# A GRU on one core: filler matmuls ahead of z's product in step 0, and smaller loads at the start

## The chip, the cores and the metric

One core of a Trainium2 chip runs the program. The metric is device time in microseconds (us), the median of several executions. The engines are named as in the profile: PE is TensorE (matmuls; PEld its weight loads), DVE is VectorE, ACT is ScalarE, POOL is GpSimd, SP is SyncE, which issues nearly all DMAs. A "q" behind an engine's name means its instruction queue.

## The reference

A gated recurrent unit runs over 128 time steps of `x` with 64 batch rows and 512 features, and its states are added to `x`:

```python
def step(h, inp):
    x_t, prop = inp
    comb = jnp.concatenate([x_t, h], axis=-1)
    z = jax.nn.sigmoid(comb @ Wz + bz)
    r = jax.nn.sigmoid(comb @ Wr + br)
    comb2 = jnp.concatenate([x_t, r * h], axis=-1)
    h_cand = jnp.tanh(comb2 @ Wh + bh)
    h_new = (1.0 - z) * h + z * h_cand
    h_next = jnp.where(prop, jnp.tanh(h_new @ Wp + bp), h_new)
    return (h_next, h_new)
# result: x + the sequence of h_new
```

`prop` holds at every fourth step but the last. Each of Wr, Wz, Wh is 1024 x 512 float32: the upper 512 rows meet x (input weights), the lower 512 meet h or r*h (state weights).

## The kernel before

A 64 x 512 state is kept as a tile of 128 partitions and 256 columns: the two halves of the features lie one below the other (`S = 2`, `B = 64`, `N = 256`). Before it can be multiplied, a tile is turned: `turn` makes eight small transposes on PE for both of its column blocks (`C = 2`) and another engine copies the result out of PSUM. `turn_x(t)` does that for step t's x, with ACT as the copying engine unless another is given.

`product(ps, lT, w, k)` is the unit of matrix work: one 128-row block k of a weight against one turned block, as two matmuls for the two halves, which the profile shows as four matmul records. A product over a whole weight takes four units in the order `ORDER = [0, 2, 1, 3]`.

What depends on x alone does not depend on the recurrence. It is cut into units that stand in `queue`, and `fill(n)` runs the next n of them, so that PE has work while the other engines bring r, z and h along. A list's last unit leaves a closure in `pending`; `read_out()` runs it, which adds the biases on DVE and writes the sums to `cp` (L435 and L440). For steps 0 to 3 the units are `plain(t)`: four of r, four of z, four of the candidate (gate order R, Z, H_). From step 4 on a scheme with fewer multiplications (Strassen-like, over several steps) is used. It needs sums of weight blocks, which DVE and POOL make during steps 0 to 2: `sum_outer` (L319 to L321, six DVE operations), `sum_outer_1` (L325), `sum_inner` (L328 to L330, on POOL) and `sum_inner_1` (L333).

One step issues, in program order on each engine: r's product (`rc`), r's sigmoid on ACT (L751) and `rh = r * h` on DVE (L752); z's product (`zp`) with the turn of rh before its last unit; z's sigmoids on ACT (L775, L776) and `keep = (1 - z) * h` on DVE (L777); `fill(places[0])`; the candidate's product into `rc`; `read_out`; tanh on ACT (L808), `h = z * tanh + keep` on DVE (L809, L814); five units of filler; the turn of h's two halves, with one unit between them; the other units. `seed` (L410) copies the x part of a sum into PSUM before a product is added to it. In step 0 `sum_outer` stands in DVE's order right after `keep`, before `read_out` and h.

The order on each engine is the program's order (`manual_schedule`), and an engine waits in order. At the start SP issues the loads in the order in which they are written:

```python
    for i in (Z, H_):
        for k in (0, 2):
            load_w(wx[:, :, i, :], gates_in[i], k, k + 2, nc.sync)
    ...
    for i in range(3):
        for k in (0, 2):
            load_w(wh[i], gates_in[i][D:, :], k, k + 2, nc.sync)
        if i == 0:
            load_x(xr[0], 2, 2, 2)
```

Here `wx` holds the input weights, `wh[i]` the state weights of gate i, and `xr[0]` the first four steps of x. `load_x` (L95) makes two DMAs, one for each half of the features; `load_w` (L100) makes one. Ahead of these lines come steps 0 and 1 of x (L115) and r's input weights in four loads of 256 KB. Behind them come `load_xs` (L157, sixteen loads of another layout of x for steps 4 to 11), Wp, bp and the next x. SP's loads share eight semaphores in turn: a load is issued when the load eight places ahead of it has landed.

Of the kernel before, what the change touches and what calls it, by code (L numbers as in the profile page):

```python
# [17 lines left out]
def kernel(  # L18
# [29 lines left out]
    nc = tc.nc  # L48
    B, T, D = x.shape
# [10 lines left out]
    R, Z, H_ = range(3)  # L60
# [21 lines left out]
    wx = const.tile([P, K, 3, H], F32, name="wx")  # L82
    wh = [const.tile([P, K, H], F32, name=f"wh_{i}") for i in range(3)]
# [4 lines left out]
    gates_in = (Wr, Wz, Wh)  # L88
# [4 lines left out]
    def load_x(tile_, t0, n, j=0):  # L93
        for s in range(S):
            nc.sync.dma_start(  # L95
                out=tile_[s * B : (s + 1) * B, j : j + n, :], in_=x[:, t0 : t0 + n, ts(s, N)]
            )

    def load_w(wt, w, k0, k1, eng):
        eng.dma_start(  # L100
            out=wt[:, k0:k1, :],
            in_=w[k0 * P : k1 * P, :].rearrange("(k p) n -> p k n", p=P),
        )

    ORDER = [s * C + c for c in range(C) for s in range(S)]
    xr = {}
# [10 lines left out]
        )  # L117
    for k in ORDER:
        load_w(wx[:, :, R, :], Wr, k, k + 1, nc.sync)
    for i in (Z, H_):  # L120
        for k in (0, 2):
            load_w(wx[:, :, i, :], gates_in[i], k, k + 2, nc.sync)

    def load_bias(i, eng):
        for s in range(S):
# [12 lines left out]
    for s in range(S):  # L138
        nc.gpsimd.dma_start(out=h_init[s * B : (s + 1) * B, :], in_=h0[:, ts(s, N)])
    for i in range(3):  # L140
        for k in (0, 2):
            load_w(wh[i], gates_in[i][D:, :], k, k + 2, nc.sync)
        if i == 0:
            load_x(xr[0], 2, 2, 2)

    dummy = const.tile([1, 1], F32, name="dummy")
    nc.scalar.activation(dummy, ones[:, 0:1], AF.Sigmoid)
# [74 lines left out]
    def products(ps, lhs, rhs, start=False):  # L222

        for s in range(S):
            nc.tensor.matmul(  # L225
                ps[s * B : (s + 1) * B],
                lhsT=lhs,
                rhs=rhs(s),
                start=start,
                stop=True,  # L230
                skip_group_check=True,
            )

    def product(ps, lT, w, k, start=False):
        s0, c0 = divmod(k, C)
        products(ps, lT[:, c0, ts(s0, B)], lambda s: w[:, k, ts(s, N)], start)
# [4 lines left out]
    def turn(src, dst, c, name, eng):  # L241


        pt = turn_ps[c][:, :P].bitcast(BF16).rearrange("p (w n) -> p w n", w=2)
        for s in range(S):
            words = src[:, c * P + s * B : c * P + (s + 1) * B].bitcast(BF16)
            for w in range(2):
                nc.tensor.transpose(  # L248
                    pt[s * B : (s + 1) * B, w, :],
                    words.rearrange("p (n w) -> p w n", w=2)[:, w, :],  # L250
                    ident16,
                )
        copy(
            eng,
            dst[:, c, :].bitcast(U16).rearrange("p (n w) -> p n w", w=2),
            pt.bitcast(U16).rearrange("p w n -> p n w"),
        )
# [7 lines left out]
    def new_xT(g):  # L265
        if g not in xT:
            xT[g] = xtp.tile([P, Q4, C, P], F32, tag="xT", name=f"xT_{g}")

    def turn_x(t, eng=nc.scalar):
        g, i = divmod(t, Q4)  # L270
        new_xT(g)
        src = xr[g]
        for c in range(C):
            turn(src[:, i, :], xT[g][:, i], c, f"xT_{t}", eng)
# [141 lines left out]
    def fill(n):  # L416
        for _ in range(min(n, len(queue))):
            unit, end = queue.pop(0)
            unit()
            if end is not None:  # L420
                pending.append(end)
# [5 lines left out]
    def plain(t):  # L427

        first, second = scratch[:2] if t % 2 == 0 else scratch[2:]
        regions = (first[:, :N], first[:, N:], second[:, :N])  # L430
        g, i = divmod(t, Q4)

        def end():
            new_cp(t // 2)
            nc.vector.tensor_add(  # L435
                G[t][:, :, 0:2, :],
                first.rearrange("p (g c n) -> p c g n", g=2, c=C),
                bias[:, :, 0:2, :],
            )
            nc.vector.tensor_add(G[t][:, :, 2, :], cut(second[:, :N]), bias[:, :, 2, :])  # L440


        order = [(e, k) for e in range(3) for k in ORDER]
        if t == Q4 - 1:
            order = [(e, k) for k in ORDER for e in range(3)]
        units = [
            lambda e=e, k=k: product(
                regions[e], xT[g][:, i], wx[:, :, e, :], k, k == ORDER[0] and e != Z
            )
            for e, k in order  # L450
        ]
        return [(u, None) for u in units[:-1]] + [(units[-1], end)]
# [113 lines left out]
    def batches(g):  # L566

        if g * Q4 >= T:
            return []
        ms = [(g, i) for i in (1, 2, 6, 5, 7, 3, 4)]  # L570
        if g + 1 < LAST:
            ms += [(g + 1, i) for i in (1, 6, 2, 5, 3, 7, 4)]
        return sum((batch((g, n), ms[2 * n : 2 * n + 2]) for n in range(7) if 2 * n < len(ms)), [])
# [103 lines left out]
    for t in range(T):  # L677
# [6 lines left out]
        places = PLACES[u]  # L684
        if t == 0:
            queue.extend(plain(2) + plain(3))
            places = (12, 12)
        elif t == 1:
            queue.extend(batch((1, 0), [(1, 1), (1, 2)]))
            places = (8, 6)  # L690
        elif t == 2:
            queue.extend(batch((1, 1), [(1, 10), (1, 11)]) + batch((1, 2), [(1, 8), (1, 9)]))
            places = (12, 8)
        elif t == 3:
            queue.extend(batches(FIRST))
            places = (8, 8, 6)
        elif u == 7:

            queue.extend(batches(even + 2))
        thin = t >= T - 9  # L700
        if thin:

            places, behind = TAIL[t - (T - 9)]
        if t == T - 10:
# [7 lines left out]
            places = (4, 5)  # L712
# [13 lines left out]


        for k in ORDER:
            product(slots[R], hT, wh[R], k)
        if t < 2:  # L730
            if t == 0:
                turn_x(2)
        if t == 1:
            for i in (5, 7):
                sum_inner(i, nc.gpsimd)
# [19 lines left out]
            seed(H_, t)  # L755
        join(0)

        if t in (2, 3):
            fill((16, 6)[t - 2])


        for k in ORDER[: 2 if thin else 3]:
# [133 lines left out]
        n = 0  # L896
        if t >= T - CHUNK:
            n = {T - 2: 3, T - 1: 1}.get(t, 0)
        elif j == Q4 - 1:
            n = 4  # L900
# [56 lines left out]
```

## Time and profile before

| | |
|---|---|
| median of 3 runs | 1329.04 us (1328.59 to 1329.49) |
| the profiled execution | 1330.24 us, its span 1328.5 us |
| granted clock of TensorE, mean | 0.999 |
| busy: PE, DVE, ACT, POOL | 1319.2, 750.8, 554.4, 881.5 us |
| HBM read, written | 43.00 MB, 16.78 MB |

The span runs from the first to the last instruction; the execution's own time also holds what lies around it. A busy PE is not a PE at its peak, since matmuls are pipelined and their ends are modelled: one shown with 379 ns is followed by the next after about 108 ns. The timeline gives the start, the length, then engine, line, operation and tiles, and in brackets the idle time before it with what ended it.

### The profile page before, as it was taken

How to read it: one execution, taken by the hardware profiler on the slowest of the kernel's cores; microseconds unless marked ns; L12 is line 12 of the kernel's file. 1: busy time of each engine (PE TensorE's matmuls, PEld its weight loads, DVE VectorE, ACT ScalarE, POOL GpSimd, SP SyncE). 2: the span in 40 equal slices, each digit the busy share in tenths (PEclk: the TensorE clock that was granted, in tenths of full speed). 3: DMA queues.
4: the chain of work that ended last, by engine and by line, in shares of the span. 5: the costliest groups of instructions: out<-in, count | busy, mean ns of one | idle time of the engine just before them, and what ended most of it. 6: DMA issues, size and time to landing. Idle time of an engine off the chain costs nothing.

```text
span 1328.5 us, 37727 instructions
## 1 busy us (share of the span) xinstructions
PE 1319.2 (99%) x15312; PEld 1117.0 (84%) x15312; DVE 750.8 (57%) x2000; ACT 554.4 (42%) x1733; POOL 881.5 (66%) x1032
## 2 busy tenths in 40 slices
PE   9999999999999999999999999999999999999998
PEld 5888888888888888888888888888888888888865
DVE  3655555555555555555555555555555555555544
ACT  1344444444444444444444444444444444444433
POOL 4876766766767577675777757676676676757530
PEclk9999999999999999999999999999999999999999
DMA  8421122121121221222111221212212112121030
GB/s 236 90 50 30 21 49 49 33 49 34 33 49 33 54 45 18 49 43 56 33 33 34 50 49 34 47 20 49 49 34 49 34 33 49 33 49 33 18 104 17
DMA packets 171438, 62.22 MB, mean 47 GB/s; under 512 B 133600, under 2 KB 166496, under 8 KB 171264
## 3 DMA queue, kind: packets, MB, share of 16 engines
q1 hardware_dynamic: 170880, 59.47, 20.8%
q8 instruction: 121, 1.98, 0.6%
q14 instruction: 53, 0.43, 0.1%
q10 hardware_dynamic: 224, 0.20, 0.1%
q0 software_dynamic: 160, 0.14, 0.0%
HBM read 43.00 MB, written 16.78 MB: 45 GB/s over the span
## 4 chain that ended last, share of the span: by engine, by line
PE 96%; SPq 1%; DMA 1%; DVE 0%; issue 0%; ACT 0%; DVEq 0%; ACTq 0%
PE rc L225 33%; PE zp L225 20%; PE scratch_q L225 11%; PE scratch_r L225 11%; PE scratch_x L225 11%; PE scratch_a L225 5%; PE turn L248 5%; DMA xr<-in_x_dram 1%; SPq L157 1%; SPq L100 0%; DMA bias<-in_L_cond_bp_dram 0%; DVE wx L333 0%; DVE turn L809 0%; SPq L115 0%; DVE xT L281 0%
## 5 line engine op out<-in xcount | busy, mean ns | idle before, releaser
L225 PE MATMUL rc<-wh,rhT 128*64 128x256 f32 x2048 | 246.0, 379 | 0.0
L580 POOL TENSOR_TENSOR cp<-mb,mb 128x768 f32<-128x768 f32 x75 | 136.3, 1818 | 107.4 <-ACT rc L410 47.5
L225 PE MATMUL zp<-wh,hT 128*64 128x256 f32 x1536 | 204.6, 379 | 0.0
L225 PEld LDWEIGHTS rc<-wh,rhT 128*64 128x64 f32 x2048 | 168.6, 137 | 40.1
L225 PE MATMUL rc<-wh,hT 128*64 128x256 f32 x1536 | 186.5, 383 | 0.4
L891 POOL TENSOR_TENSOR xr<-xr,h 128x256 f32<-128x256 f32 x127 | 92.7, 730 | 126.3 <-DVE h L814 126.3
L225 PEld LDWEIGHTS rc<-wh,hT 128*64 128x64 f32 x1536 | 122.3, 137 | 36.1 <-issue 10.1
L580 POOL TENSOR_TENSOR cp<-mb 128x768 f32<-128x768 f32 x47 | 85.3, 1815 | 94.7 <-DVE h L814 89.8
L225 PEld LDWEIGHTS zp<-wh,hT 128*64 128x64 f32 x1536 | 119.7, 137 | 24.7
L809 DVE TENSOR_TENSOR turn<-turn,z 128x128 f32<-128x128 f32 x256 | 75.4, 295 | 102.2 <-ACT turn L808 100.7
L239 DVE COPY rhT<-turn 128x256 uint16<-128x256 uint16 x256 | 97.6, 420 | 56.0 <-PE turn L248 51.6
L751 ACT ACTIVATE turn<-rc 128x128 f32<-128x128 f32 x256 | 55.3, 260 | 171.4 <-issue 113.8
L239 ACT COPY hT<-turn 128x256 uint16<-128x256 uint16 x127 | 47.3, 373 | 165.5 <-DVE hT L239 130.7
L548 DVE TENSOR_TENSOR mb<-scratch_r,cq 128x384 f32<-128x384 f32 (+1 forms) x107 | 59.3, 554 | 91.8 <-ACT cq L547 90.3
L580 POOL TENSOR_TENSOR mb<-mb,mb 128x768 f32<-128x768 f32 x58 | 105.4, 1817 | 8.5 <-DVE mb L550 8.5
L541 DVE TENSOR_TENSOR cx<-scratch_r,cx 128x384 f32<-128x384 f32 (+1 forms) x107 | 59.3, 554 | 88.0 <-ACT cx L539 88.0
L775 ACT ACTIVATE z<-zp 128x256 f32<-128x256 f32 x128 | 49.2, 384 | 136.7 <-PE zp L225 136.7
L410 ACT COPY rc<-cp 128x256 f32<-128x256 f32 x256 | 96.4, 377 | 18.3 <-DVE cp L435 4.6
L808 ACT ACTIVATE turn<-rc 128x128 f32<-128x128 f32 x256 | 55.2, 260 | 112.8 <-PE rc L225 111.7
L814 DVE TENSOR_TENSOR h<-turn,keep 128x128 f32<-128x128 f32 x254 | 74.1, 292 | 15.2
L248 PEld LDWEIGHTS <-h 128*64 128x64 bf16 x1016 | 68.1, 110 | 12.2 <-DVE h L814 6.5
L248 PE MATMUL turn<-ident,h 128*64 128x128 bf16 x1016 | 77.8, 220 | 0.3 <-DVE h L814 0.3
(165 smaller groups left out, 2931.7 us busy)
## 6 DMA issues: line engine op xcount, KB each, us to landing
xs<-in_x_dram SPq DMA_DIRECT2D x248, 64.0 KB, 2.8
xr<-in_x_dram SPq DMA_DIRECT2D x62, 256.0 KB, 4.1
out_dram<-xr SPq DMA_DIRECT2D x62, 256.0 KB, 3.3
wx<-in_L_cond_Wr_dram SPq DMA_DIRECT2D x7, 256.0 KB, 4.5
wx<-in_L_cond_Wz_dram SPq DMA_DIRECT2D x2, 512.0 KB, 6.4
wx<-in_L_cond_Wh_dram SPq DMA_DIRECT2D x2, 512.0 KB, 9.5
wh<-in_L_cond_Wr_dram SPq DMA_DIRECT2D x2, 512.0 KB, 12.7
wh<-in_L_cond_Wz_dram SPq DMA_DIRECT2D x2, 512.0 KB, 13.0
```

Of the source, the lines that this page charges most:

```text
L225: nc.tensor.matmul(ps[s * B : (s + 1) * B], lhsT=lhs, rhs=rhs(s), start=start, stop=True, skip_group_check=True,)
L239: (eng.copy if eng is nc.scalar else eng.tensor_copy)(dst, src)
L248: nc.tensor.transpose(pt[s * B : (s + 1) * B, w, :], words.rearrange("p (n w) -> p w n", w=2)[:, w, :], ident16,)
L410: nc.scalar.copy(cut(slots[i]), G[t][:, :, i, :])
L541: nc.vector.tensor_add(T2[n][:, :nm], r_ps[:, :nm], T2[n][:, :nm])
L548: nc.vector.tensor_add(blocks()[:, :nm, 0, 1], r_ps[:, :nm], q2[:, :nm])
L580: nc.gpsimd.tensor_add(dst, a, b)
L751: nc.scalar.activation(act_ps[c], slots[R][:, ts(c, P)], AF.Sigmoid)
L808: nc.scalar.activation(pc, slots[H_][:, ts(c, P)], AF.Tanh)
L809: nc.vector.tensor_mul(pc, pc, z[:, ts(c, P)])
L814: nc.vector.tensor_add(h_new[:, ts(c, P)], pc, keep[:, ts(c, P)])
L891: nc.gpsimd.tensor_add(xr[g][:, j, :], xr[g][:, j, :], h_new)
```

## The change

In the order of SP's loads: the candidate's input weights are loaded in four DMAs of 256 KB in the order of `ORDER` instead of two of 512 KB. r's state weights likewise. Of x's steps 2 and 3, which were loaded together behind r's state weights, step 2 stays there and step 3 goes behind z's state weights; each is two DMAs of 64 KB where there were two of 128 KB for both. Six DMAs more are issued.

In step 0: `turn_x(2)` goes from behind r's product to in front of its fourth unit. Eight of the twelve units that ran behind z's product run in front of it; four stay.

```diff
-    for i in (Z, H_):
-        for k in (0, 2):
-            load_w(wx[:, :, i, :], gates_in[i], k, k + 2, nc.sync)
+    for k in (0, 2):
+        load_w(wx[:, :, Z, :], Wz, k, k + 2, nc.sync)
+    for k in ORDER:
+        load_w(wx[:, :, H_, :], Wh, k, k + 1, nc.sync)
...
     for i in range(3):
-        for k in (0, 2):
-            load_w(wh[i], gates_in[i][D:, :], k, k + 2, nc.sync)
-        if i == 0:
-            load_x(xr[0], 2, 2, 2)
+        for n, k in enumerate(ORDER):
+            if i == R:
+                load_w(wh[i], gates_in[i][D:, :], k, k + 1, nc.sync)
+            elif n % 2 == 0:
+                load_w(wh[i], gates_in[i][D:, :], n, n + 2, nc.sync)
+        if i < H_:
+            load_x(xr[0], 2 + i, 1, 2 + i)
...
         if t == 0:
             queue.extend(plain(2) + plain(3))
-            places = (12, 12)
+            places = (4, 12)
...
         for k in ORDER:
+            if t == 0 and k == ORDER[3]:
+                turn_x(2)
             product(slots[R], hT, wh[R], k)
-        if t < 2:
-            if t == 0:
-                turn_x(2)
...
-        if t in (2, 3):
-            fill((16, 6)[t - 2])
+        if t in (0, 2, 3):
+            fill((8, 0, 16, 6)[t])
```

## The prediction

> **What bounds the kernel now.** I read the page first, then the waits of TensorE, then the timelines of TensorE, VectorE and GpSimd over the first 46 us, because every line of the diff acts before or inside step 0.
>
> ```profile
> span 1328.5 us, 37727 instructions
> PE 1319.2 (99%) x15312; PEld 1117.0 (84%) x15312; DVE 750.8 (57%) x2000; ACT 554.4 (42%) x1733; POOL 881.5 (66%) x1032
> ```
>
> TensorE works nearly all the time, so any idle time of it goes straight into the span, and there is little of it to win. The change cannot touch more than the stalls of the start-up. The waits of TensorE name them (total, times, longest), and its timeline shows their places (start, length, then the idle time in brackets):
>
> ```profile
> PE zp L225 <- DMA wh<-in_L_cond_Wz_dram: 1.4, 2, 0.8
> PE rc L225 <- DMA wh<-in_L_cond_Wr_dram: 0.4, 1, 0.4
> ```
> ```profile
> 15.51 0.60 PE L225 MATMUL scratch_r<-wx,xT 128*64 128x256 f32 x4
> 16.38 1.52 PE L225 MATMUL scratch_r<-wx,xT 128*64 128x256 f32 x12 [0.27 <-DMA wx<-in_L_cond_Wh_dram]
> ...
> 19.46 0.60 PE L225 MATMUL rc<-wh,hT_init 128*64 128x256 f32 x4
> 20.43 1.51 PE L225 MATMUL rc<-wh,hT_init 128*64 128x256 f32 x12 [0.38 <-DMA wh<-in_L_cond_Wr_dram]
> 21.78 0.41 PE L248 MATMUL turn<-ident,xr 128*64 128x128 bf16 x8
> 22.78 0.65 PE L225 MATMUL zp<-wh,hT_init 128*64 128x256 f32 x4 [0.60 <-DMA wh<-in_L_cond_Wz_dram]
> 24.21 1.08 PE L225 MATMUL zp<-wh,hT_init 128*64 128x256 f32 x8 [0.78 <-DMA wh<-in_L_cond_Wz_dram]
> ```
>
> A unit (one `product`) has four matmul records and takes 0.43 us: the 32 records of scratch_q run from 25.78 to 29.23, which is 8 x 0.43. The brackets count from the modelled end of a matmul, so I measure from the start expected. The second scratch_r unit was due at 15.94 and came at 16.38: 0.44 lost. The second rc unit was due at 19.89 and came at 20.43: 0.54. The eight transposes of a turn take 0.22 (30.96 to 31.18 for the next x), so z's product was due at 22.00 and came at 22.78: 0.78. Its second unit was due at 23.21 and came at 24.21: 1.00. Sum 2.76 us, or 0.21% of the span: all that this change could ever bring.
>
> The other half of the picture is VectorE, in the same step:
>
> ```profile
> 26.69 0.42 DVE L777 TENSOR_TENSOR keep<-zp,h_init 128x256 f32<-128x256 f32 x1 [0.48 <-ACT zp L776]
> 27.03 0.95 DVE L319 TENSOR_TENSOR tw<-wx 128x768 f32<-128x768 f32 x1
> ...
> 32.74 0.69 DVE L435 TENSOR_TENSOR cp<-scratch_q,bias 128x512 f32<-128x512 f32 x1
> ...
> 33.99 0.29 DVE L814 TENSOR_TENSOR h<-turn,keep 128x128 f32<-128x128 f32 x1
> ...
> 35.74 2.62 DVE L325 TENSOR_TENSOR wx<-wx 128x768 f32<-128x768 f32 x2
> ```
>
> VectorE has no idle time from keep to the new h. The six sums of `sum_outer` stand between the two in its program, with two sums for step 2 behind them. h was there at 34.28 and TensorE turned it at 35.07, because only then had it finished its filler: a slack of 0.74 us once 0.05 is taken off for the signal (rh of the next step ended at 41.57 in the chain and its turn began at 41.61).
>
> **The change part by part.** *Candidate's input weights in four loads.* The unit due at 15.94 needs row block 2, which shared a 512 KB load with block 3 and landed at 16.38. Now it is in the second of four loads, and blocks 1 and 3 are needed 0.43 and 0.86 later. Block 3 still lands at 16.3 and is needed at 16.8. Gain 0.44.
>
> *r's state weights in four loads.* The rc product now begins at 19.02. The first half of these weights was in by 18.84 (SyncE's first xs issue waited for it), the second at 20.4. Blocks 0 and 2 are in the first half now, and block 1, about halfway at 19.6, is needed at 19.88. The 0.54 goes. TensorE reaches the moved turn of x at 20.31.
>
> *The turn of step 2's x before r's fourth unit.* What is late next is x itself. Its first 128 KB load landed at 21.21 (the longest piece in the chain, 7.75 plus 13.46); its second was in by 21.78, when the old turn ran. Both loads are now half as big, behind the same weights, which end at 20.4. The bounds are 20.31 (no wait) and 21.78 (no gain); I take 21.0, nearest to half of the way from 20.4 to 21.7. The turn then costs 0.22 and the fourth unit runs to 21.65. ScalarE's copy of the first half of x started 0.33 after the old turn and took 0.37 (0.65 for both, partly overlapped), so the first filler unit can run at 21.75.
>
> *Eight units in front of z's product.* 8 x 0.43 = 3.45, to 25.20. They hide the 1.78 us of waits for z's weights, which landed at 22.78 and 24.21 and now have less x in front of them. If that cover failed, it would cost as much as z's weights came after 25.20. They also hide r's sigmoid and rh. Then come z's three units (1.30), the turn of rh (0.22) and the last unit (0.43): z's sum is complete at 27.15, against 25.78 before. So z is **1.37 later**, while TensorE still has less work between z and the candidate: four filler units instead of twelve.
>
> *VectorE behind z.* From the end of z's product to the first half of h it took 34.28 - 25.78 = 8.50, without a gap after keep. That gives 35.65, and a turn of h at 35.70 against 35.07. TensorE gets there at 27.15 + 1.73 (four units) + 0.22 (turn of step 3's x) + 1.73 (candidate) + 2.16 (five units) = 32.99 and **stands idle for 2.7 us**. All of the saving is lost in this new wait, and 0.63 more. The rest of step 0, step 1's product and every engine behind h queue behind that turn.
>
> *After h.* VectorE's L325 took 1757 ns for its first part while GpSimd's L333 ran, and 948 for its second part alone. First GpSimd's timeline, then the chain of work that ended last:
>
> ```profile
> 35.80 1.76 POOL L333 TENSOR_TENSOR tw<-tw 128x384 f32<-128x384 f32 x1
> ```
> ```profile
> 41.36 0.21 DVE rh L752
> 41.57 0.04 issue
> ```
>
> GpSimd's sums follow `sum_outer`, so they move by 1.37, and L325 only by 0.63, to 36.37. It now meets the end of L330 (36.21 to 37.21, 1.00 long) and then L333. Bounds: 0.8 gained if it met neither, 1.0 lost if it waits for one operation more; I take 0.3 lost, since one meeting is there already. This stretch of VectorE sets step 1's rh: the turn at 41.61 was due at 41.35, so a loss passes on in full, and of a gain only 0.27 can be used.
>
> For the same place the Trainium skill, "SBUF — State Buffer", section "Who interferes with whom", says that a VectorE operation with two SBUF inputs and a GpSimd one that reads SBUF exclude each other, and that the later one blocks fully. By that rule alone L325 would be held to 37.21, or to 38.2 if L333 went first, and the term would be 0.0 to 1.0, the median 1329.7 to 1330.7.
>
> *Edits at nothing.* Six more loads on SyncE, about 0.5 us of issue each: SyncE waits there anyway for the load eight places ahead (4.4 us on Wh, 1.6 on Wz). Behind them queue the xs loads, wanted at 39.77; the last of both groups was issued by 33.03 and lands in 2.8 at the median. Step 3's x, behind z's weights, is wanted at 28.9, after those landed at 24.2. Candidate's state weights are wanted at 29.1. The sum of step 2 needs its twelve units by 34.1 and has them at 28.9.
>
> **Sum.** +0.63 + 0.30 = +0.93 us. The profiled execution took 1330.24 (span 1328.5 and 1.7 around it), 1.2 over the median of 1329.04, so 1331.2 for such an execution and 1330.0 for the median. With x at 20.31 and the 0.27 gained it is -0.3; with x at 21.78 and the full 1.0 it is +2.4: 1328.7 to 1331.4.
>
> **The rivals.** *The clock falls in the new gap.* The longest stall before is about 1 us and the granted clock stays at full. At the start TensorE ran at half rate from 1.20 to 4.6 us (512-column matmuls 0.427 apart, then 0.216). If 2.7 us of idleness brings that back, 3.4 us at half rate costs 1.7, twice that 3.4: 1331.7 to 1333.4, **slower**. Against it: the gap is shorter than the 3.4 us that the start took; for it: the profile shows no gap as long that was survived. The Trainium skill, "TensorE: Matmul & The Clock Gate", section "Why this matters for your kernels", asks for no gap above some 3 us. By that rule this gap just passes and the sum stays at 1330.0; half a microsecond more and it would not.
>
> *The smaller loads come later.* With eight loads in flight, four of 256 KB and two of 64 KB hold fewer bytes than before, and x is issued later. Each microsecond that x lands after 21.0 moves everything behind it by one; it decides against the change from 20.4 on. For 1 to 2 us it is 1331.0 to 1332.0. Against it: weights were issued 13 us before they landed.
>
> *The intended gain arrives.* If h did not wait for VectorE, the 2.76 would go less x's 0.7 and the copy's 0.1: 1327.1, and 1326.3 if x is in time. For it: each removed wait is real. Against it: the operations between keep and h are fixed in VectorE's order and have no gap.
>
> **How the numbers follow.** The forecast has 0.65, the clock 0.14, the late loads 0.11, the gain 0.10. What a measurement of this kernel can tell from no change is about 0.2%, 2.66 us: below 1326.4 or above 1331.7. Faster: the best third of the gain, 0.03. Slower: the clock's case (0.13), the last third of the late loads (0.03), the end of the forecast's unknowns (0.02): 0.18. The rest, 0.79, is within. The range 1327.5 to 1332.4 leaves out a good half of the gain (0.06) and the upper half of the clock's case (0.07), and something for what I have not seen.
>
> **What would show it.** In the profile after: no TensorE idle at scratch_r and rc before 20.3; a short wait for xr in front of the turn; none at z's product; z's sigmoid near 27.4; VectorE's six sums from 28.4; a TensorE wait of 2 to 3 us for h at 33 to 36, which is the step that decides; the turn of h at 35.7; step 1's turn of rh near 42.5. I am wrong if TensorE waits for h less than 1 us, if the matmuls after that gap are spaced at twice 0.108, or if x comes after 22.

## The result: 0.2 % slower, and the profile after

After the change the median is **1331.95 us** (18 runs, 1331.68 to 1332.07); the kernel before, run beside it, has **1329.32 us** (18 runs, 1327.96 to 1330.80). The ratio is 1.002, with a 95% interval of 1.0014 to 1.0026: 2.63 us more. The interval leaves out 1.000, so the change is slower, but by no more than the 0.2% (2.66 us) that the prediction took for the least that counts as a difference. The profiled execution took 1331.81 us against 1330.24, 1.57 more. One thing in these numbers matters later: the runs of before are spread over 2.8 us, those of after over 0.4.

The head of the page of the kernel after:

```profile
span 1330.0 us, 37738 instructions
PE 1320.2 (99%) x15312; PEld 1118.5 (84%) x15312; DVE 751.9 (57%) x2000; ACT 555.0 (42%) x1733; POOL 880.1 (66%) x1032
```

The waits of TensorE after (total, times, longest). The waits for `wh` that stood here are gone; a wait for h is new and is the largest:

```profile
PE turn L252 <- DVE h L817: 2.8, 2, 2.6
PE rc L217 <- DVE zeros L73: 1.2, 1, 1.2
PE scratch_r L229 <- DVE mb L552: 0.2, 1, 0.2
```

Its timeline (start, length, idle time in brackets) shows the place:

```profile
15.49 1.90 PE L229 MATMUL scratch_r<-wx,xT 128*64 128x256 f32 x16
...
18.95 1.47 PE L229 MATMUL rc<-wh,hT_init 128*64 128x256 f32 x12
20.24 0.39 PE L252 MATMUL turn<-ident,xr 128*64 128x128 bf16 x8
20.46 0.60 PE L229 MATMUL rc<-wh,hT_init 128*64 128x256 f32 x4
21.00 3.67 PE L229 MATMUL scratch_q<-wx,xT 128*64 128x256 f32 x32
24.50 1.47 PE L229 MATMUL zp<-wh,hT_init 128*64 128x256 f32 x12
...
30.13 1.03 PE L229 MATMUL scratch_a<-wx,xT 128*64 128x256 f32 x8
30.99 0.60 PE L229 MATMUL scratch_x<-wx,xT 128*64 128x256 f32 x4
31.43 1.03 PE L229 MATMUL scratch_a<-wx,xT 128*64 128x256 f32 x8
35.01 0.31 PE L252 MATMUL turn<-ident,h 128*64 128x128 bf16 x4 [2.55 <-DVE h L817]
...
35.99 1.93 PE L229 MATMUL scratch_a<-wx,xT 128*64 128x256 f32 x8
...
42.99 0.39 PE L252 MATMUL turn<-ident,rh 128*64 128x128 bf16 x8
```

The same two turns before:

```profile
35.07 0.28 PE L248 MATMUL turn<-ident,h 128*64 128x128 bf16 x4
...
41.61 0.51 PE L248 MATMUL turn<-ident,rh 128*64 128x128 bf16 x8
```

Nearly every start from 15.49 to 31.43 follows from the one before it, and no row shows idle time: 16 records take 1.73, 12 take 1.3, a turn 0.22. Only scratch_q at 21.00 starts 0.11 late, behind the copy of x, for which the prediction took 0.1. Before, there were 2.76 us of holes in this stretch. Then TensorE stands for 2.55 us and turns h at 35.01. Before it was 35.07. So the whole saving but 0.06 us ends in one wait. The row at 35.99 shows a second loss: the eight records of scratch_a take 1.71 until the next row (37.70) where the eight at 30.13 took 0.86. Step 1's turn of rh comes at 42.99 against 41.61, and this 1.4 stays up to the end.

VectorE after, from keep on, and GpSimd beside it:

```profile
27.36 0.42 DVE L780 TENSOR_TENSOR keep<-zp,h_init 128x256 f32<-128x256 f32 x1 [0.48 <-ACT zp L779]
27.70 0.95 DVE L323 TENSOR_TENSOR tw<-wx 128x768 f32<-128x768 f32 x1
...
33.41 0.68 DVE L439 TENSOR_TENSOR cp<-scratch_q,bias 128x512 f32<-128x512 f32 x1
...
34.66 0.29 DVE L817 TENSOR_TENSOR h<-turn,keep 128x128 f32<-128x128 f32 x1
...
35.73 3.24 DVE L329 TENSOR_TENSOR wx<-wx 128x768 f32<-128x768 f32 x2
```
```profile
35.50 1.00 POOL L334 TENSOR_TENSOR tt<-tw,tt 128x384 f32<-128x384 f32 x1
36.45 1.71 POOL L337 TENSOR_TENSOR tw<-tw 128x384 f32<-128x384 f32 x1
```

VectorE has no gap from keep to h, as before; the chain starts 0.67 later (keep was at 26.69). L329, the old L325, takes 3.24 where it took 2.62, because it now begins inside GpSimd's L334 and then meets L337 as well.

The windows of after say what happened to the matmuls behind the gap (stretch, then busy time of PE, PEld, DVE, ACT and POOL, then PEclk, the granted clock, then the busy share of the DMA engines and what they moved in GB/s):

```profile
32.00:35.00 3.00, 0.46 (x6) 0.00 (x1) 2.93 (x7) 0.00 (x0) 2.35 (x2) 1.00 0.95 234
35.00:37.00 2.00, 1.99 (x18) 1.28 (x20) 1.97 (x4) 0.37 (x1) 1.92 (x3) 0.59 1.08 358
37.00:39.00 2.00, 2.00 (x14) 1.18 (x12) 2.00 (x3) 0.00 (x0) 1.16 (x1) 0.55 0.94 184
39.00:41.00 2.00, 2.00 (x22) 1.32 (x20) 2.00 (x6) 0.00 (x0) 0.00 (x0) 1.00 0.02 5
```

The clock was granted in full until the gap, fell to about half right behind it, and was back at 39. The loss is 2 x 0.41 + 2 x 0.45 = 1.72 us of full-rate work. Before, every one of these windows shows 1.00.

### The profile page after: what moved, and what is told of

The parts are those of the page before. It is cut to its first block, busy times and chain, and to the rows that moved or that the text cites. A ratio compares the mean times of both kernels' runs of the same rounds, so it can differ in the third digit from the quotient of the medians.

```text
span 1330.0 us, 37738 instructions
## 1 busy us (share of the span) xinstructions
PE 1320.2 (99%) x15312; PEld 1118.5 (84%) x15312; DVE 751.9 (57%) x2000; ACT 555.0 (42%) x1733; POOL 880.1 (66%) x1032
## 4 chain that ended last, share of the span: by engine, by line
PE 99%; DVE 1%; issue 0%; ACT 0%; DVEq 0%; ACTq 0%
PE rc L229 34%; PE zp L229 21%; PE scratch_q L229 11%; PE scratch_x L229 11%; PE scratch_r L229 11%; PE scratch_a L229 6%; PE turn L252 5%; PE rc L217 0%; PE zp L217 0%; DVE tw L324 0%; DVE tw L323 0%; DVE turn L812 0%; PE scratch_x L200 0%; DVE tw L325 0%; DVE h L817 0%
```

## The experiments

The theory after the result: VectorE's chain behind z (keep, six sums, two cp, h) sets the turn of h; the eight units delay z and through it this chain; the gap then drops the clock; the loads matter only to what runs ahead of that. The rivals: the smaller loads cost something themselves; the clock's fall is free because VectorE is late anyway; the gap has another cause than the six sums. Each kernel ran 11 times, beside the kernel before (medians 1328.9 to 1329.3).

### How the time goes with the number of units in front of z

The kernel is the change itself, with all its other edits.

```diff
-            places = (4, 12)
+            places = (12, 12)
...
-            fill((8, 0, 16, 6)[t])
+            fill((0, 0, 16, 6)[t])
```

This is e1, with no unit in front of z and twelve behind it. In e2 the numbers are 2 and 10, in e3 6 and 6.

> The changed kernel with no unit in front of z's product (all twelve behind it); loads and x's turn as changed. Theory 'wait for h, then the clock' (VectorE needs some 8.56 us from z's end to h, TensorE idles for it, and that idle time drops its clock for 3.4 us): z's product ends near 23.4 with about 0.4 us of wait for z's weights; h is ready before TensorE wants it; no clock drop; the turn of h near 32.7; about 3.5 us under the changed kernel, 1328.4. Rival 'the smaller loads cost the time': the loads are the same, so it stays at 1331.5 to 1332.

> As changed, but two units in front of z's product and ten behind. Theory 'wait for h, then the clock': z's weights are just covered, the wait for h is about 0.1 us, no clock drop, turn of h near 32.4; VectorE is then the bound of step 1's rh; about 3.8 us under the changed kernel, 1328.1, the best of the row. Rival 'the smaller loads cost the time': 1331.5 to 1332.

> As changed, but six units in front of z's product and six behind. By 0.432 us for a unit the wait for h shrinks from 2.7 to 1.86 us and h's turn comes near 34.1. If the clock stays up after so short a wait: about 2.1 us under the changed kernel, 1329.85. If the clock falls after it too: 0.9 under, 1331.05. Rival 'the smaller loads cost the time': 1331.5 to 1332.

| units in front of z | median, us | ratio to before | turn of h | L329's two | turn of rh, step 1 |
|---|---|---|---|---|---|
| 0 (e1) | 1328.41 | 0.9996 (0.9987 to 1.0005) | 33.04 | 2.62 | 39.58 |
| 2 (e2) | 1328.78 | 0.9998 (0.9989 to 1.0007) | 32.92 | 3.26 | 40.16 |
| 6 (e3) | 1330.32 | 1.0012 (1.0003 to 1.0020) | 34.26 | 3.25 | 41.48 |
| 8 (the change) | 1331.95 | 1.002 (1.0014 to 1.0026) | 35.01 | 3.24 | 42.99 |

Without the eight units the change costs nothing: the loads and the early turn of x are not what makes it slower. The misses of e2 (0.7 above what was expected) and e3 (0.5) have a cause in common, which I had not counted: once VectorE's chain sets the turn of h, L329 starts well inside L334 and takes 3.25, and TensorE waits for rh in step 1. In e2 the turn of h also came 0.5 later than expected (32.92 for 32.4), and TensorE had waited 0.4 for z's weights. The waits of e3:

```profile
PE turn L252 <- DVE h L817: 2.0, 2, 1.7
...
PE turn L252 <- DVE rh L755: 0.8, 1, 0.8
```

The windows of e3 behind its wait of 1.7 us show no fall of the clock, against 0.59 and 0.55 behind 2.55 us. This is one execution; the slowest of the other runs of e3 took 1331.34, 1.0 above their median, and has no profile.

```profile
35.00:37.00 2.00, 2.00 (x24) 1.35 (x22) 2.00 (x3) 0.37 (x1) 2.00 (x2) 1.00 1.02 373
37.00:39.00 2.00, 2.00 (x22) 1.32 (x20) 2.00 (x3) 0.00 (x0) 0.42 (x1) 1.00 1.08 223
```

### What the fall of the clock costs

The change, with 22 matmuls of zeros in front of the turn of h, added into a buffer where they alter nothing. They keep TensorE at work while VectorE's chain stays as it is.

```diff
+        if t == 0:
+            for i in range(22):
+                s = i % S
+                nc.tensor.matmul(
+                    scratch[3][s * B : (s + 1) * B, N:],
+                    lhsT=zeros[:, :B],
+                    rhs=zeros[:, :N],
+                    start=False,
+                    stop=True,
+                    skip_group_check=True,
+                )
```

> The changed kernel with 22 matmuls of zeros (64 x 256, bf16, added to an unused half bank) in front of the turn of h in step 0: TensorE works instead of idling, but h comes no sooner. Theory 'wait for h, then the clock': h's turn stays at 35.0, the clock does not fall, the 1.7 us of half speed go, and VectorE's sums behind h become the bound of step 1's rh (0.6 back): about 1.1 us under the changed kernel, 1330.85. Rival 'the wait alone, the clock costs nothing because VectorE is late anyway': 1331.9. Rival 'the smaller loads': 1331.9.

Measured: 1331.16 us, ratio 1.0017 (1.0008 to 1.0026). TensorE's timeline in e4, and a window of it:

```profile
32.43 1.37 PE L826 MATMUL scratch_x<-zeros 128*64 128x256 bf16 x22
35.15 0.31 PE L252 MATMUL turn<-ident,h 128*64 128x128 bf16 x4 [1.35 <-DVE h L817]
...
42.38 0.51 PE L252 MATMUL turn<-ident,rh 128*64 128x128 bf16 x8 [0.77 <-DVE rh L755]
```
```profile
35.00:37.00 2.00, 1.85 (x24) 1.24 (x26) 1.97 (x5) 0.37 (x1) 1.92 (x3) 1.00 1.00 357
```

The zeros filled only half of the gap, but that was enough: the clock stayed at 1.00. The turn of h did not come sooner, so the gap is VectorE's and not TensorE's. From there to step 1's turn of rh it now takes 7.23 where the change took 7.98. The fall of the clock is worth 0.75 in the trace and 0.79 in the medians: less than half of its 1.72, because behind a full clock TensorE waits 0.77 for rh, which L329 makes late. The two medians come from different sessions, in which the kernel before had 1329.32 and 1328.88, but the ranges of the two kernels do not meet (1330.99 to 1331.53 against 1331.68 to 1332.07). The rival that the fall is free is out, and so is its full price.

### Take the sums out of VectorE's chain

The change, with the six sums of `sum_outer` (and GpSimd's behind them) issued right behind rh, ahead of the filler, instead of behind keep.

```diff
         join(0)
+        if t == 0:
+            sum_outer()
+            for i in (6,):
+                sum_inner(i, nc.gpsimd)
+                sum_inner_1(i, nc.gpsimd)
         if t in (0, 2, 3):
             fill((8, 0, 16, 6)[t])
...
-        if t == 0:
-            sum_outer()
-            for i in (6,):
-                sum_inner(i, nc.gpsimd)
-                sum_inner_1(i, nc.gpsimd)
```

> The changed kernel with sum_outer (and GpSimd's sum_inner(6) behind it) issued right after rh instead of after keep, in the 4 us in which VectorE waits for the turn of rh; eight units stay in front of z's product. Theory 'the six sums between keep and h make the wait': h is ready before TensorE wants it, its turn comes at 32.3 instead of 35.0, no idle time and no clock drop, GpSimd's sums no longer meet L329, step 1's rh sets nothing: the turn of rh near 38.6 against 42.99, some 4.4 us under the changed kernel, 1327.5, and faster than before by 1 us or more. Rival 'eight units in front of z make h late whatever VectorE does' : h's turn stays near 35, 1331 to 1332.

Measured: 1328.74 us, ratio 0.9994 (0.9985 to 1.0003), 3.2 us less than the change. The gap and the fall of the clock are gone, and L329 meets nothing:

```profile
33.47 0.31 PE L252 MATMUL turn<-ident,h 128*64 128x128 bf16 x4
```
```profile
34.16 1.82 DVE L329 TENSOR_TENSOR wx<-wx 128x768 f32<-128x768 f32 x2
```

That is the theory's main test. But the median lies 1.2 above what was expected. In the waits of e5 something else is late:

```profile
PE turn L252 <- DMA h_init<-in_cond_dram: 1.0, 1, 1.0
PE turn L252 <- DVE h L817: 0.3, 1, 0.3
```

I put the miss down to this load of h_init and, with the sums where e5 has them, issued it sooner:

```diff
-    nc.gpsimd.tensor_copy(held, wx[0:1, 1, R, 0:1])
+    nc.gpsimd.tensor_copy(held, wx[0:1, 0, R, 0:1])
```

> The change with the six sums of the outer weights ahead of VectorE's wait for z (as in e5), and with GpSimd's `held` copying from row block 0 of r's input weights instead of block 1, so that the load of h_init is issued 1 to 2 us sooner. In e5 the turn of h_init waited 1.02 us for the second half of h_init, and everything behind it moved by that. Theory (VectorE's chain between z and h made the gap; with the sums taken out of it TensorE is the bound again, and h_init's late load is all that e5 still lost): no wait at h_init, turn of h at 32.4 to 32.5, no idle time for h above 0.5 us, turn of rh of step 1 at 38.7, median 1327.5 to 1327.9. Rival (the weights' loads set the start whatever h_init does, as their spread did in e7): a wait for weights or for x takes the place of h_init's and the median stays at 1328.5 to 1328.8.

Measured: 1328.52 us, ratio 0.9996 (0.9987 to 1.0005). The wait for h_init was gone, and the median fell by only 0.2, with the kernel before at 1329.01 beside e5 and 1328.96 beside e9: my reading was wrong. VectorE's and TensorE's timelines of e9 show why:

```profile
27.56 0.96 DVE L325 TENSOR_TENSOR tw<-wx,tw 128x768 f32<-128x768 f32 x1
28.44 0.75 DVE L243 COPY rhT<-turn 128x256 uint16<-128x256 uint16 x2
```
```profile
28.91 0.64 PE L252 MATMUL turn<-ident,xr 128*64 128x128 bf16 x8 [0.44 <-DVE rhT L243]
29.35 1.95 PE L229 MATMUL rc<-wh,rhT 128*64 128x256 f32 x16
```

rhT's copies now queue behind all six sums. TensorE's own order would have begun the candidate at 28.52; it begins at 29.35, 0.83 later. In e5 the late h_init had hidden this: the candidate began at 29.57 there. So the last sum went back behind keep (`sum_outer` now takes the numbers of the sums to do, 0 to 5):

```diff
         if t == 0:
-            sum_outer()
-            for i in (6,):
-                sum_inner(i, nc.gpsimd)
-                sum_inner_1(i, nc.gpsimd)
+            sum_outer(range(5))
...
         nc.vector.tensor_mul(keep, slots[Z], h)
+        if t == 0:
+            sum_outer(range(5, 6))
+            for i in (6,):
+                sum_inner(i, nc.gpsimd)
+                sum_inner_1(i, nc.gpsimd)
```

> As e9, but only five of the six sums of the outer weights stand ahead of rhT's copies on VectorE; the sixth, and GpSimd's sums behind it, stand behind keep. In e9 the gap for h was gone, but rhT's copies queued behind all six sums (28.44), and TensorE turned x's step 3 at 28.91 where its own order gave 28.30, and began the candidate at 29.35 where it gave 28.52: 0.83 lost. Theory (it is VectorE's order at this place that sets step 0, whichever tile waits behind the sums): rhT's copies at 27.5, candidate at 28.5, turn of h at 32.4 to 32.5, and since VectorE has no slack behind h but everything moves with it, the turn of rh of step 1 at 38.7 to 38.9: 0.7 to 0.8 below e9, median 1327.7 to 1327.9. Rival (the time is given back behind h, by L329 meeting GpSimd's sums or by a wait at rh): turn of h at 32.4 but turn of rh of step 1 at 39.4 or later, median 1328.4 or more.

Measured: **1327.57 us** (1327.29 to 1327.95), ratio 0.9987 (0.9978 to 0.9996). It is 1.8 us below the kernel before and 4.4 below the change, and faster than before by a little more than its uncertainty, though by less than the 0.2% named above. VectorE and TensorE in e10:

```profile
27.96 0.75 DVE L243 COPY rhT<-turn 128x256 uint16<-128x256 uint16 x2
...
33.47 1.82 DVE L333 TENSOR_TENSOR wx<-wx 128x768 f32<-128x768 f32 x2
```
```profile
28.87 1.95 PE L229 MATMUL rc<-wh,rhT 128*64 128x256 f32 x16
...
32.78 0.31 PE L252 MATMUL turn<-ident,h 128*64 128x128 bf16 x4
...
39.05 0.42 PE L252 MATMUL turn<-ident,rh 128*64 128x128 bf16 x8
```

No row of TensorE shows idle time in step 0, and step 1's turn of rh is 3.9 us ahead of the change. The candidate begins 0.35 later than expected (28.87 for 28.5), and the turn of h with it; the median is a shade lower than expected all the same. By TensorE's own order (z's product ended at 26.69) the candidate was due at 28.64, so 0.23 of e9's loss of 0.83 is left: moving one sum back brought 0.60 at this place. How much of e10's gain over the kernel before would remain with the old loads was not tried.

### The loads

The kernel before with one part of the change each: e6 only runs the eight units in front of z; e7 only loads x's steps 2 and 3 apart; e8 only loads r's state weights and the candidate's input weights in four.

```diff
-            places = (12, 12)
+            places = (4, 12)
...
-        if t in (2, 3):
-            fill((16, 6)[t - 2])
+        if t in (0, 2, 3):
+            fill((8, 0, 16, 6)[t])
```
```diff
-        if i == 0:
-            load_x(xr[0], 2, 2, 2)
+        if i < H_:
+            load_x(xr[0], 2 + i, 1, 2 + i)
```
```diff
...
+    for k in ORDER:
+        load_w(wx[:, :, H_, :], Wh, k, k + 1, nc.sync)
...
+            if i == R:
+                load_w(wh[i], gates_in[i][D:, :], k, k + 1, nc.sync)
```

> The kernel before with only the eight units moved in front of z's product (the turn of step 2's x where it was, the old loads). Theory 'wait for h, then the clock': the waits at scratch_r and rc stay, those at z's product go; z ends near 27.4, h's turn near 36, with the same idle time of 2.7 us and the same clock drop; as late as the changed kernel or up to 1 us later, 1332 to 1333. Rival 'the loads of the change cost the time': 1329.

> The kernel before with only x's steps 2 and 3 loaded apart (step 3 behind z's weights). If x's loads slow the others down while they run (the reason why the changed kernel's x was there 0.8 us before I had it): z's weights land 1 us or more sooner and all of it counts, 1327.5 to 1328. If only their bytes count: 0.4 us sooner, 1328.5.

> The kernel before with only the four loads of 256 KB for the candidate's input weights and for r's state weights. The waits at scratch_r (0.44) and rc (0.54) go, and the waits for z's weights, which land no sooner, take them back: 1328.9, no change. If the smaller loads are what brought everything sooner in the changed kernel, z's weights land 1 us or more sooner: 1327.9.

Measured: e6 1332.11 us (1.0019, 1.0010 to 1.0028), e7 1328.87 (0.9995, 0.9986 to 1.0004), e8 1329.39 (1.0001, 0.9992 to 1.0010). e6 is as slow as the change, has the same wait of 2.6 for h, and its windows show the same fall of the clock, further on with its gap:

```profile
35.00:37.00 2.00, 1.02 (x16) 0.70 (x18) 1.93 (x8) 0.12 (x1) 1.84 (x3) 1.00 1.02 357
37.00:39.00 2.00, 2.00 (x14) 1.12 (x12) 2.00 (x2) 0.26 (x1) 2.00 (x2) 0.58 1.11 299
39.00:41.00 2.00, 2.00 (x14) 1.16 (x12) 2.00 (x4) 0.00 (x0) 0.15 (x1) 0.57 0.54 110
```

The eight units alone thus make the whole loss, and with them the loads buy nothing. One part of what was expected did not come: the waits at scratch_r and rc, which were to stay in e6 with its old loads, are not in its profile. Alone the loads cannot be told from no change either; e7 is 0.4 above the higher of its two expected values, e8 0.5 above its own. First the waits of e8, then that of e7, whose r and candidate weights are loaded as before:

```profile
PE zp L229 <- DMA wh<-in_L_cond_Wz_dram: 1.3, 2, 0.7
...
PE turn L252 <- DMA xr<-in_x_dram: 0.2, 1, 0.2
```
```profile
PE zp L225 <- DMA wh<-in_L_cond_Wz_dram: 0.3, 1, 0.3
```

In e8 the waits at scratch_r and rc are gone, and z's weights are as late as before, so TensorE waits there instead. The profiled execution of e7 took 1327.60, with 0.3 us of waits for z's weights and none for weights at scratch_r or rc; that of before took 1330.24, with 1.4 and 0.4 at zp and rc. The other runs of e7 reach 1330.04. So how long TensorE waits for the first weights seems to differ from run to run by as much as these edits move it; only one execution of each kernel was profiled.

## Why the prediction was right, and where it was not

*The mechanism was right.* The stalls went, z became later, TensorE met a gap for h of 2.55 (2.7 forecast), and h was not earlier. e1, e4, e5 and e6 show each link: without the units no loss; with TensorE kept busy the same turn of h; without the sums in the chain no gap; with the units alone the whole loss.

*But the median does not lie where the forecast's own terms put it.* 1331.95 is above their bounds (1328.7 to 1331.4) and just inside those of the clock's rival (1331.7 to 1333.4). One of the three signs of being wrong came true: the matmuls behind the gap are spaced at twice 0.108 (1.71 for eight). The other two did not. That the median fell among the rival's numbers, and inside the range, is partly luck: the clock brought only 0.8, and the step to the median, below, brought 1.34, while x, sooner by 0.7, took off as much.

*x came sooner than I took.* The turn of x ran at 20.24 without a wait, where I took 21.0 between 20.31 and 21.78. z's product ended at 26.45 (27.15 forecast), and h was turned at 35.01 (35.70). From the end of z's product to the turn of h it took 8.56, forecast 8.55. The +0.63 at the turn of h was -0.06.

*L329's meeting was too small.* +0.62 for the 0.30 that I took, of a bound of 1.0. I had also read the two parts of L325 before in the wrong order:

```profile
L325 DVE TENSOR_TENSOR wx<-wx x2: 948/1352/1757, 35.7 to 36.6; 128x768 f32<-128x768 f32 x2
```

The second part starts 0.9 behind the first, so the first took 948 ns, what a part takes alone (e5, e10), and the second 1757, while L333 ran. In the change the parts took 1575 and 1745: the second meets L337 as before, and the first is new in meeting L334, which had 0.77 still to run. A part that meets a GpSimd operation ends some 0.8 us behind that one's end: 37.31 behind 36.50 and 38.97 behind 38.16 in the change, 38.36 behind 37.56 before. So the price follows from how much of L334 is left when L329 begins: 3.24 to 3.26 with 0.77 left (the change, e2, e3, e4), 2.71 with 0.22 (e7, where the lines are L325 and L330), 2.62 with 0.1 (before, e1), 1.82 with no meeting (e5, e10). By the rule of the Trainium skill ("SBUF — State Buffer", "Who interferes with whom"), by which the two engines shut each other out, I had put it between 0.0 and 1.0. These ends agree with one engine waiting for the other.

*The clock's rival did happen, beside the forecast.* I gave it 0.14 and 1.7 us as if it excluded the forecast. It came in at a gap of the forecast length, and its price was 0.8, not 1.7, since rh was late in any case: two losses on parallel engines do not add. "TensorE: Matmul & The Clock Gate" in the Trainium skill ("Why this matters for your kernels") asks for no gap above some 3 us. By that rule the prediction let this gap pass. Here 2.55 us was too much, in the change and in e6, and in the profiled executions 1.7 (e3) and 1.35 (e4) were not. The measurement decides.

*The sum, in the profiled executions.* Forecast +0.93; measured +1.57. Put right by the terms above, -0.69 for x, +0.32 for L329 and +0.75 for the clock, the 0.93 becomes +1.31. The remaining 0.26 I have not traced.

*The step from the profiled execution to the median was the largest error.* I took 1.2 off, because before's profiled execution lay that far above its median, as if after's would do so too. After's lies 0.14 below: a difference of 1.34, of the 1.95 by which the median missed 1330.0. Before's profiled execution was one with late weights; e7 shows one with early ones, and e6, whose weights are loaded as before, began rc at nearly the same time (19.49 against 19.46) and did not wait there. So part of the 2.76 us that I set out from was probably this execution's and not the kernel's. The runs of the change spread over 0.4 us. That VectorE's chain sets step 0 there does not explain it: e6, with the same wait for h and the old loads, spreads over 1.3, and e1, with the new loads and the early turn of x but without the wait, over 0.4. The kernels with the new loads and the early turn spread over 0.4 to 1.4, e7 and e8 with a part of the loads each over 2.4 and 2.0. What makes the time so steady was not tried by itself. The time lies in that part of the range that was put there for the clock.

*The late loads and the intended gain* did not occur. The second is what e10 brings, with VectorE's order changed too.

## What to carry to other kernels

Before you fill a stall of one engine with work from further on, ask which chain on another engine begins at the work that you delay: here z, and behind it six sums that nobody needed yet. Work that is wanted late belongs in an engine's idle time ahead of the critical operation, and only as much of it as fits: one sum too many cost 0.6 us in e9. And when the profiled execution lies off the median, find out whether the part that you remove is the reason, before you carry the offset over.

## What the runs showed of the hardware that I had not expected

- The granted clock fell to about half for some 3.4 us (1.72 us lost at half rate) after TensorE had been idle for 2.55 us (after and e6), and stayed up behind 1.7 and 1.35 us (e3, e4). In after the fall begins within the first window behind the gap; in e6 the gap ends at 35.98 and the window up to 37 still shows 1.00. Whether the length of the gap or also its place decides was not tried.
- 22 matmuls of zeros of 256 columns took 1.37 us in the trace, about half of the gap that they were put into.
- Two equal VectorE operations in a row took 1.82 us alone and up to 3.26 with GpSimd operations beside them; each one that met a GpSimd operation ended some 0.8 us behind its end.
